# Layer 3: inverse deviations by way of 128 partitions, and one minus the offset's size on ScalarE

## The chip, the cores and the metric

The kernel runs on one core of a Trainium2 chip. The metric is the device time of one execution in microseconds (us), as the median of several runs. The engines are named as in the profile: PE (TensorE), PEld (its weight loads), DVE (VectorE), ACT (ScalarE), POOL (GpSimd) and SP (SyncE, which here issues transfers only).

## What is computed

Four layers run one after another on a tensor of 8 images, 256 channels and 32 x 32 pixels: an attention block with an MLP (layer 0), a bottleneck with a deformable convolution (layer 1), a binarised convolution with a batch normalisation (layer 2), and a second deformable convolution block (layer 3). The change touches layer 3 alone. In the reference (cut):

```python
h = silu(bn(conv2d(x, w_cv1, 1, 1), ...))                 # 3x3, 256 -> 128 channels
t = conv2d(h, w_dw, 1, 1, groups=128) + b_dw              # depthwise 3x3
t = gelu(layernorm(t over the 128 channels, ln_g, ln_b))  # (t - mean) * rsqrt(var + eps) * g + b
value = h @ w_inp + b_inp
offset = t @ w_off + b_off                                # 4 groups x 9 taps x (x, y)
mask = softmax(t @ w_msk + b_msk over the 9 taps)
o = dcnv3_core(value, offset, mask)                       # bilinear samples of value, weighted by mask
return x + silu(bn(o @ w_out + b_out))
```

## The kernel before

Channels lie on the 128 partitions, pixels along the free dimension. Layer 3 works image by image (b = 0 to 7), and each image in two halves of 512 pixels (h = 0, 1).

**The front of an image.** The normalised output of layer 2 is added to x and copied into a padded tile. PE convolves it (`convolve3`, 18 taps a half, L1284), ACT applies SiLU (`silu`, L1289). The depthwise convolution is one tap on ACT (`depthwise`, L1307) and eight on DVE (L1310). For the layer norm PE subtracts the mean by a matmul (`centered`, L1319), ACT squares and copies (L1325, L1327), and PE sums the squares in `variances` (L1333): four matmuls put the variances of 256 pixels each on 32 equal rows, so that the tile `rs` (128 x 256) holds 1024 different numbers, each 32 times. ACT takes the root (`deviations`, L1339), DVE the reciprocal of the whole tile (`inverse`, L1342). PE spreads rows 0, 32, 64 and 96 of it over all channels (`inverse_spread`, L1348; `pick` is zero for the other rows), DVE multiplies (`scaled`, L1352), ACT applies GELU (`gelu`, L1355). PE makes offsets and masks (`offsets3`, L1361), and DVE adds their bias (L1368).

**From offsets to weights.** No pixel is gathered. Offsets here are below 1 in size, so a bilinear sample is a sum over the 3 x 3 pixels around the tap, and with the 9 taps over 25 shifts. `hats` makes the three hat functions of an offset: its absolute value (ACT, L1380), the positive parts of both signs (ACT, L1382, L1384), the largest absolute value for a final test that offsets are indeed below 1 (DVE, L1386), and one minus the absolute value (DVE, L1388). `masks` is the softmax (L1400 to L1409; exponentials on ACT). `weights` multiplies and adds them up into 25 weights per pixel and group: `mx`, `pt`, `ws` on POOL (L1421, L1424, L1427), for image 0 on DVE. `parts` splits them into three bf16 parts (ACT L1438, DVE L1436), PE transposes them (L1447), ACT copies (L1452).

**The products.** For each half and each of the 25 shifts PE spreads a weight over the channels (`shift_weights`, `pw`, L1457, three PSUM banks), DVE multiplies it with the shifted values (`product`, `pr`, L1466, six buffers), and the products are added up: most on POOL (`add_pool`, L1481 for the first addition of a half and L1483), the others on PE (`add_helper`, L1475) or DVE (L1471). The two sums meet in `add_both` (`ab`, DVE, L1486). `outward` (PE, L1490), SiLU (`outward_silu`, ACT, L1495), `add_input` (`oi`, POOL, L1500) and a store on SP (L1503) end the half.

**What sets the order.** A planner in the kernel, `Order`, sets the order of the work on all engines when the program is built. Each piece has an engine, an estimated time, a rank, the pieces that it comes after, the buffers that it takes and gives, and a lag until another engine sees its end. The planner takes whichever piece can start first by these estimates, and of several the one with the lowest rank; a switch of ACT's function table counts 1.28 us. PE, ACT, DVE and POOL then execute in exactly this order, each waiting at its next instruction until what it needs is there; SP executes its transfers in order too. The pieces around the change read:

```python
piece(("dev", b), "ACT", 0.48, r, [("var", b)], deviations, b, give=["ps"], kind="sqrt")
piece(("inv", b), "DVE", 1.74, r, [("dev", b)], inverse, b)
for h in range(2):
    piece(("is", b, h), "PE", 0.86, r, [("inv", b)], inverse_spread, b, h, take=["ps"])
    piece(("sc", b, h), "DVE", 0.68, r - 500, [("is", b, h), ("zc", b, h)], scaled, b, h, give=["ps"])
```

Here r is 100 b; the products have rank 100 b + 150.

Layer 0 has transfers within SBUF of a like kind, to which the prediction turns for a price: `lay` (L499) copies a row block of sums to other partitions, and L436 puts small blocks of eight rows into one row.

Of the kernel before, what the change touches and what calls it, by code (L numbers as in the profile page):

```python
# [8 lines left out]
F32 = mybir.dt.float32  # L9
# [3 lines left out]
AF = mybir.ActivationFunctionType  # L13
ALU = mybir.AluOpType
# [4 lines left out]
P = 128  # L19
# [31 lines left out]
QP = N // 4  # L51
# [107 lines left out]
def conv_seq_kernel(ctx: ExitStack, tc: tile.TileContext, d: dict, out: bass.AP):  # L159
    nc = tc.nc  # L160
# [75 lines left out]
    with ExitStack() as s0:  # L236
        w = s0.enter_context(tc.tile_pool(name="a_w", bufs=1))
# [343 lines left out]
        for n, m in enumerate(blocks):  # L581
            b, g, h = m
# [79 lines left out]
    with ExitStack() as s1_:  # L662
        w = s1_.enter_context(tc.tile_pool(name="b_w", bufs=1))
# [42 lines left out]
        one = s1_.enter_context(tc.tile_pool(name="b_one", bufs=1))  # L706
# [15 lines left out]
        def piece(key, engine, time, rank, after, f, *args, take=(), give=(), lag=Order.LAG):  # L722
            T[key] = work.add(engine, time, rank, [T[a] for a in after if a in T], lambda: f(*args), take, give, lag)
# [315 lines left out]
        for b in range(B):  # L1039
            r = 100 * b  # L1040
# [18 lines left out]
            r = 100 * b - 50  # L1059
# [51 lines left out]
        b = B - 1  # L1111
# [21 lines left out]
        b = B - 1  # L1133
        for o in range(2):
            piece(("vu", o), "PE", 3.9, 100 * b + 330, [("x", b, 0, 0), ("x", b, 1, 0), ("h", b, 1, 7)], convolve_upper, b, o, 0, take=["pm"])
        for h in range(2):
            for o in range(2):
                k = b, o, h
                r = -200 + 10 * h + o
# [21 lines left out]
    with ExitStack() as s3_:  # L1161
        w = s3_.enter_context(tc.tile_pool(name="d_w", bufs=1))
# [30 lines left out]
        identb = w.tile([P, P], BF16, name="identb")  # L1193
        group = w.tile([P, G3], F32, name="group")
        silu_in = w.tile([P, 1], F32, name="silu_in")

        def constants():
            nc.vector.tensor_scalar_add(center, ident, -1.0 / P)
            nc.vector.memset(mean_w, 1.0 / P)
            nc.vector.memset(pick, 0.0)  # L1200
            for j in range(4):
                nc.vector.memset(pick[32 * j : 32 * j + 1, j % 2, :], 1.0)
            nc.vector.tensor_copy(identb, ident)
# [9 lines left out]
        one = s3_.enter_context(tc.tile_pool(name="d_one", bufs=1))  # L1213
# [29 lines left out]
        T, S = {}, {}  # L1243
# [93 lines left out]
        def deviations(b):  # L1337
            S["rs", b] = one.tile([P, QP], F32, name="rs")
            nc.scalar.activation(S["rs", b], S.pop(("var", b))[:, :QP], AF.Sqrt, bias=eps)  # L1339

        def inverse(b):
            nc.vector.reciprocal(S["rs", b], S["rs", b])  # L1342

        def inverse_spread(b, h):
            S["is", b, h] = bank3()
# [27 lines left out]
        def hats(b, i):  # L1373

            off = S["om", b][:, :, : 2 * GK]
            if i == 0:
                S["hat", b] = one.tile([P, 3, NT, 2 * GK], F32, name="hat")
            hat = S["hat", b]
            if i == 0:
                nc.scalar.activation(hat[:, 1], off, AF.Abs)  # L1380
            elif i == 1:
                nc.scalar.activation(hat[:, 0], off, AF.Relu, scale=-1.0)  # L1382
            elif i == 2:
                nc.scalar.activation(hat[:, 2], off, AF.Relu)  # L1384
            elif i == 3:
                nc.vector.tensor_reduce(largest[:, b : b + 1], hat[:, 1].rearrange("p t o -> p (t o)"), AX.X, ALU.max)  # L1386
            else:
                nc.vector.tensor_scalar(hat[:, 1], hat[:, 1], -1.0, 1.0, ALU.mult, ALU.add)  # L1388

        def masks(b, i):  # L1390

# [113 lines left out]
        for b in range(B):  # L1505

            r = 100 * b
# [6 lines left out]
            if b == 0:  # L1514
                piece("arrange", "DVE", 1.7, 20, [("a", 0, 1, 1)], arrange)
                piece("constants", "DVE", 2.0, 20, [("a", 0, 1, 1)], constants)
                for i in range(SB):
                    piece(("sel", i, 0), "DVE", 0.4, 60, ["constants"], spread_rows, i, 0, take=["spread"])
                    piece(("sel", i, 1), "PE", 0.25, 60, [("sel", i, 0)], spread_rows, i, 1, take=["ps"], give=["spread"])
                    piece(("sel", i, 2), "DVE", 0.25, 60, [("sel", i, 1)], spread_rows, i, 2, give=["ps"])  # L1520
                piece("silu", "ACT", 0.2, r, [("xp", 0, 1)], nc.scalar.activation, silu_in, eps, AF.Silu, kind="silu")
            last = ("c", b - 1, 1, 1, 8)
            for h in range(2):
                for t in range(2):
                    for k in range(9):
                        c = b, h, t, k
# [15 lines left out]
                piece(("zc", b, h), "ACT", 0.6, r, [("zs", b, h)], centered_copy, b, h, 1, give=["ps"])  # L1542
            piece(("var", b), "PE", 0.8, r, [("zs", b, 0), ("zs", b, 1)], variances, b, take=["ps"])
            piece(("dev", b), "ACT", 0.48, r, [("var", b)], deviations, b, give=["ps"], kind="sqrt")
            piece(("inv", b), "DVE", 1.74, r, [("dev", b)], inverse, b)
            for h in range(2):
                piece(("is", b, h), "PE", 0.86, r, [("inv", b)], inverse_spread, b, h, take=["ps"])
                piece(("sc", b, h), "DVE", 0.68, r - 500, [("is", b, h), ("zc", b, h)], scaled, b, h, give=["ps"])
# [8 lines left out]
            piece(("ms", b, 4), "DVE", 0.8, r, [("ms", b, 3)], masks, b, 4)  # L1557
            for i in range(3):
                piece(("ha", b, i), "ACT", 0.67, r, om + [("ha", b, i - 1)], hats, b, i)
            piece(("ha", b, 3), "DVE", 0.72, r + 90, [("ha", b, 0)], hats, b, 3)  # L1560
            piece(("ha", b, 4), "DVE", 0.54, r, [("ha", b, 3)], hats, b, 4)
            piece(("w", b, -1), "POOL", 0.9, r, om, weights, b, -1, 0)
            ready = [("ms", b, 4), ("w", b, -1)] + [("ha", b, i) for i in (1, 2, 4)]
            last = []
# [15 lines left out]
            r = 100 * b + 150  # L1580
# [44 lines left out]
    with tc.If(nc.values_load(flag[0:1, 0:1]) > 0):  # L1625
        with ExitStack() as s3_:
            w = s3_.enter_context(tc.tile_pool(name="d_w", bufs=1))
# [25 lines left out]
            one = s3_.enter_context(tc.tile_pool(name="d_one", bufs=1))  # L1653
# [210 lines left out]
```

## Time and profile before

| | us |
|---|---|
| median of 3 runs (4552.45 to 4561.46) | 4553.63 |
| profiled execution: its own time | 4538.69 |
| profiled execution: span of the core | 4536.9 |
| busy in the span: PE / DVE / ACT / POOL | 4030.8 / 3065.7 / 1857.3 / 3300.6 |
| first reciprocal L1342 starts at | 3938.2 |
| first product added on POOL at | 3979.0 |

The profile is of one execution on the core; the mean granted clock of PE was 0.941 of full speed. Layer 3 fills the last 15% or so of the span, from about 3880 us on. A view names an engine, a line of the kernel, the operation and "written <- read" tiles; a number behind an x is a count, an arrow in brackets names what ended the idle time before an instruction. `pr`, `part`, `ws` and so on are names of tiles.

### The profile page before, as it was taken

Reading aid. Unit: us, or ns where it says so; the run is one execution under the profiler, and the core shown is the slowest. Engines: PE = TensorE matmul, PEld = TensorE weight load, DVE = VectorE, ACT = ScalarE, POOL = GpSimd, SP = SyncE. Lnnn points to the kernel's source line nnn. Section 1 sums busy time; section 2 is a strip of 40 time slices with the busy share of each in tenths; the row PEclk is TensorE's granted clock in tenths of the full one; section 3 lists DMA queues with packets and bytes.
Section 4 is the critical chain, followed back from the end, with each engine's and each line's share of the span. In section 5 each row is a group of like instructions: output and inputs, shape, how many; then the busy total and the mean of one; then the engine's idle time right before and its main releaser. Section 6 shows DMA issues by size and latency. Waiting matters only on the chain.

```text
span 4536.9 us, 60173 instructions
## 1 busy us (share of the span) xinstructions
PE 4030.8 (89%) x20901; PEld 1551.4 (34%) x20901; DVE 3065.7 (68%) x5201; ACT 1857.3 (41%) x3338; POOL 3300.6 (73%) x2011
## 2 busy tenths in 40 slices
PE   6999999999999999999999998777777766899977
PEld 2333333333333333333333323322233322344332
DVE  6777777777777777777777763455464554688885
ACT  2554555555555555555455542122122211534331
POOL 3889888988888888988898873554554653078787
PEclk8999999999999999999999999887788888999988
DMA  5212222222221221222222211222332332100000
GB/s 163 66 57 58 65 65 54 65 71 56 59 72 55 61 71 55 58 67 64 55 63 74 57 49 52 80 83 73 88 89 66 99 103 66 40 10 15 14 14 24
DMA packets 207143, 283.09 MB, mean 62 GB/s; under 512 B 87264, under 2 KB 117488, under 8 KB 206576
## 3 DMA queue, kind: packets, MB, share of 16 engines
q1 hardware_dynamic: 176272, 195.46, 15.4%
q0 software_dynamic: 28720, 77.90, 5.8%
q10 hardware_dynamic: 1840, 5.81, 0.3%
q8 instruction: 168, 2.75, 0.3%
q14 instruction: 143, 1.17, 0.1%
HBM read 181.07 MB, written 63.82 MB: 54 GB/s over the span
## 4 chain that ended last, share of the span: by engine, by line
PE 68%; DVE 13%; another core or an unknown queue 7%; issue 5%; POOL 5%; ACT 2%; DMA 1%; SPq 0%; DVEq 0%; POOLq 0%; ACTq 0%
PE av L460 19%; PE pb L403 11%; PE sc L448 10%; PE pb L386 5%; PE pc L1284 3%; PE pm L758 3%; PE pb L534 2%; PE po L771 2%; PE pb L330 2%; DVE near_p L935 2%; POOL part L1483 2%; PE pc L1006 2%; DVE pm L407 1%; DVE r L491 1%
## 5 line engine op out<-in xcount | busy, mean ns | idle before, releaser
L470 POOL TENSOR_TENSOR esum<-esum,e 128x1024 f32<-128x1024 f32 x762 | 1809.2, 2405 | 54.6 <-ACT e L449 54.1
L407 DVE TENSOR_REDUCE pm<-pb 128x1 f32<-128x512 f32 x2016 | 1357.3, 685 | 657.0 <-PE pb L403 653.1
L449 ACT ACTIVATE e<-sc 128x512 f32<-128x512 f32 x2048 | 1056.9, 602 | 676.3 <-PE sc L448 664.1
L460 PE MATMUL av<-e,v 128*64 128x512 f32 x4096 | 1053.4, 593 | 0.0
L913 POOL DMA_INDIRECT g<-table,idx x576 | 550.2, 955 | 562.1 <-DVE near_p L935 286.5
L403 PE MATMUL pb<-sk,sq 128*64 128x512 bf16 x4032 | 772.7, 387 | 56.3 <-DVE x L542 23.4
L448 PE MATMUL sc<-q,k 32*128 32x512 f32 x4096 | 592.9, 642 | 0.0
L403 PEld LDWEIGHTS <-sq 128*64 128x64 bf16 x4032 | 266.2, 109 | 911.0 <-issue 885.6
L468 POOL TENSOR_TENSOR esum<-e 128x1024 f32<-128x1024 f32 x127 | 303.1, 2406 | 299.0 <-ACT e L449 299.0
L460 PEld LDWEIGHTS av<-e,v 128*64 128x64 f32 x4096 | 294.7, 137 | 208.7 <-issue 117.7
L1483 POOL TENSOR_TENSOR part<-part,pr 128x512 f32<-128x512 f32 x212 | 276.1, 1302 | 54.6 <-DVE pr L1466 43.3
L771 PE MATMUL po<-hid,kept 128*128 128x512 f32 x512 | 257.6, 653 | 57.0 <-DVE x L775 41.9
L1466 DVE TENSOR_TENSOR pr<-pw,v 128x512 f32<-128x512 f32 x394 | 253.9, 682 | 63.5 <-POOL part L1483 31.8
L1284 PE MATMUL pc<-xpad,kept 128*128 128x512 f32 x576 | 276.1, 603 | 11.6 <-ACT xpad L1279 8.0
L758 PE MATMUL pm<-y,wide 128*128 128x512 f32 x512 | 247.8, 631 | 27.8 <-ACT hid L763 20.5
L534 PE MATMUL pb<-o,wp 128*64 128x512 f32 x1024 | 245.0, 597 | 1.2 <-DVE r L512 0.6
L448 PEld LDWEIGHTS sc<-q,k 32*128 32x128 f32 x4096 | 166.0, 183 | 230.1 <-issue 186.0
L386 PE MATMUL pb<-wide,y 128*64 128x256 f32 x2048 | 241.8, 379 | 0.0
L491 DVE RECIPROCAL r<-r 128x128 f32<-128x128 f32 x252 | 237.3, 942 | 0.1
L763 ACT ACTIVATE hid<-pm,vec 128x512 f32<-128x512 f32 x128 | 86.8, 686 | 284.5 <-PE pm L758 146.5
L935 DVE TENSOR_TENSOR near_p<-g,near_p 128x320 f32<-128x320 f32 (+1 forms) x384 | 177.4, 462 | 13.2
L390 ACT COPY v<-pb 128x512 f32<-128x512 f32 x128 | 75.1, 586 | 265.5 <-PE pb L386 265.5
(265 smaller groups left out, 4068.8 us busy)
## 6 DMA issues: line engine op xcount, KB each, us to landing
sq<-lev_d SPq DMA_DIRECT2D x512, 64.0 KB
r<-r SPq DMA_DIRECT2D x504, 64.0 KB
sk<-lev_d SPq DMA_DIRECT2D x496, 64.0 KB
lev_d<-lev SPq DMA_DIRECT2D x180, 128.0 KB
u_d<-u SPq DMA_DIRECT2D x60, 256.0 KB
g<-table,idx POOLq DMA_INDIRECT x576
out<-res SPq DMA_DIRECT2D x32, 256.0 KB
q<-u_d SPq DMA_DIRECT2D x124, 64.0 KB
```

Of the source, the lines that this page charges most:

```text
L386: nc.tensor.matmul(ps[c * 64 : (c + 1) * 64, (mt % 2) * 256 : (mt % 2 + 1) * 256], ys[b][:, t, k0 : k0 + 64], wv[:, t, g * 256 : (g + 1) * ...
L403: nc.tensor.matmul(ps[c * 64 : (c + 1) * 64, :], sq[pair][:, c, q0 : q0 + 64], sk[pair][:, c, kh * HALF : (kh + 1) * HALF], start=True, st ...
L407: nc.vector.tensor_reduce(maxima[m][:, pair, qt, kh : kh + 1], ps, AX.X, ALU.max)
L448: nc.tensor.matmul(ps, k[r, kt * P : (kt + 1) * P], q[r, h * HALF : (h + 1) * HALF], start=True, stop=True)
L449: nc.scalar.activation(es[m, kt, j // 2][:, j % 2, :], ps, AF.Exp)
L460: nc.tensor.matmul(av[i * HD : (i + 1) * HD, :], vss[b, g][:, kt, j * HD : (j + 1) * HD], e[:, i, :], start=kt == 0, stop=kt == NT - 1,)
L470: eng.tensor_add(sums[m, pair], sums[m, pair], es.pop((m, kt, pair)))
L758: nc.tensor.matmul(ps, w1[:, t, i * P : (i + 1) * P], ys[b, h][:, t, :], start=t == 0, stop=t == 1)
L771: nc.tensor.matmul(pss["o", b, h, t], w2[:, j, t * P : (t + 1) * P], hids[b, h, j], start=j == 0, stop=j == 7)
L913: nc.gpsimd.indirect_dma_start(out=g[:, k, :], out_offset=None, in_=tables[b][:TR, :], in_offset=bass.IndirectOffsetOnAxis(ap=idxs[b][:, t ...
L1284: nc.tensor.matmul(S["c", b, h], wc[:, t, k, :], tap(xpads[t], k, H // 2, h * H // 2), start=t == k == 0, stop=t == 1 and k == 8,)
L1483: nc.gpsimd.tensor_add(S["part", b, h], S["part", b, h], S.pop(("pr", b, h, on_pool[n])))
```

## The change

Two things change. First, the reciprocal of the deviations. `narrow` copies rows 0, 32, 64 and 96 of `rs`, each 256 numbers on one partition, onto 32 partitions of 8 numbers each (`r8`, 128 x 8), in four transfers on SP's queue. DVE takes the reciprocal of `r8`. `widen` copies the results back into the four rows, again in four transfers. Second, one minus the absolute offset is made by ACT instead of DVE, with a bias tile of ones. Ranks change with it: the new pieces have r - 500, and the maximum of the offsets has r instead of r + 90. The lines of the changed kernel lie 2 to 14 further down.

```diff
+        unit = w.tile([P, 1], F32, name="unit")
...
+            nc.vector.memset(unit, 1.0)
...
+        def narrow(b):
+            S["r8", b] = one.tile([P, QP // 32], F32, name="r8")
+            for j in range(4):
+                nc.sync.dma_start(S["r8", b][32 * j : 32 * j + 32, :], S["rs", b][32 * j : 32 * j + 1, :].rearrange("o (p c) -> o p c", p=32))
+
         def inverse(b):
-            nc.vector.reciprocal(S["rs", b], S["rs", b])
+            nc.vector.reciprocal(S["r8", b], S["r8", b])
+
+        def widen(b):
+            for j in range(4):
+                nc.sync.dma_start(S["rs", b][32 * j : 32 * j + 1, :].rearrange("o (p c) -> o p c", p=32), S["r8", b][32 * j : 32 * j + 32, :])
...
-                nc.vector.tensor_scalar(hat[:, 1], hat[:, 1], -1.0, 1.0, ALU.mult, ALU.add)
+                nc.scalar.activation(hat[:, 1], hat[:, 1], AF.Identity, bias=unit, scale=-1.0)
...
-            piece(("inv", b), "DVE", 1.74, r, [("dev", b)], inverse, b)
+            piece(("nar", b), "SP", 0.5, r - 500, [("dev", b)], narrow, b, lag=2.2)
+            piece(("iv", b), "DVE", 0.15, r - 500, [("nar", b)], inverse, b)
+            piece(("inv", b), "SP", 0.5, r - 500, [("iv", b)], widen, b, lag=2.2)
...
-            piece(("ha", b, 3), "DVE", 0.72, r + 90, [("ha", b, 0)], hats, b, 3)
-            piece(("ha", b, 4), "DVE", 0.54, r, [("ha", b, 3)], hats, b, 4)
+            piece(("ha", b, 3), "DVE", 0.72, r, [("ha", b, 0)], hats, b, 3)
+            piece(("ha", b, 4), "ACT", 0.6, r, [("ha", b, 3)], hats, b, 4)
```

Since the planner plans with these costs, the order of the pieces around them changes on all engines.

## The prediction

> **What bounds the kernel now.** The page puts layer 3 at the end of the span. I read the windows first, then POOL's and DVE's waits within the stage, then the changed lines, then the timeline of the first batch. Windows (columns: us, then busy us and instructions of PE, PEld, DVE, ACT, POOL, then granted clock):
>
> ```profile
> 4060.00:4120.00 60.00, 58.24 (x210) 27.18 (x208) 54.79 (x80) 25.91 (x33) 49.13 (x42) 1.00 0.03 9
> 4300.00:4360.00 60.00, 51.20 (x171) 22.30 (x172) 52.12 (x79) 23.47 (x29) 50.95 (x41) 0.94 0.05 18
> ```
>
> Three engines are 80 to 97% busy, ACT under half: nothing is free except on ACT. Waits of POOL and DVE, 3940 to 4537 us:
>
> ```profile
> POOL part L1481 <- DVE pr L1466: 115.3, 12, 91.5
> POOL part L1483 <- DVE pr L1466: 43.3, 48, 4.3
> ...
> DVE pr L1466 <- POOL part L1483: 31.8, 19, 11.6
> DVE pr L1466 <- PE pw L1457: 29.2, 50, 2.3
> ```
>
> 91.5 us is POOL's wait for its first product; after it POOL waits 23.8 + 43.3 = 67 us for DVE, and DVE 32 us for POOL. The bound changes hands: sometimes DVE's products are late (POOL idle 2 to 4 us), sometimes POOL adds 14 in a row and DVE waits for a buffer. The two changed lines (min/median/max ns):
>
> ```profile
> L1342 DVE RECIPROCAL rs<-rs x8: 1742/1743/1752, 3938.2 to 4383.0; 128x256 f32<-128x256 f32 x8
> ...
> L1388 DVE TENSOR_SCALAR hat<-hat x8: 460/962/1171, 3948.5 to 4425.3; 128x576 f32<-128x576 f32 x8
> ```
>
> Batch 0, timeline (start, us). Its reciprocal finds DVE idle, and the chain from it leads to the first product and so to POOL's start:
>
> ```profile
> 3937.66 0.47 ACT L1339 ACTIVATE rs<-ps,eps 128x256 f32<-128x256 f32 x1
> ...
> 3938.17 1.75 DVE L1342 RECIPROCAL rs<-rs 128x256 f32<-128x256 f32 x1 [3.57 <-ACT rs L1339]
> ...
> 3940.24 1.14 PE L1348 MATMUL ps<-rs,pick 64*128 64x256 f32 x8
> ```
> ```profile
> 3978.99 1.27 POOL L1481 TENSOR_TENSOR part<-pr 128x512 f32<-128x512 f32 x1 [91.53 <-DVE pr L1466]
> ```
>
> Layer 3 makes no such transfer, but layer 0 does: row to rows (L499) and rows to row (L436). Timeline of SP, then of POOL, which uses the last L499 transfer:
>
> ```profile
> 2376.97 2.80 SPq L436 DMA_DIRECT2D q<-line  x4
> ...
> 2686.44 4.94 SPq L499 DMA_DIRECT2D r<-r  x8
> ```
> ```profile
> 2692.98 1.27 POOL L504 TENSOR_TENSOR o<-r,o 128x512 f32<-128x512 f32 x1 [0.79 <-DMA r<-r]
> ```
>
> Four transfers of this kind cost SP 2.80 us of issue, and the reader starts 2692.98 - (2686.44 + 4.94) = 1.60 us after the last issue ends. So four together land about 4.4 us after SP may start.
>
> **What the Trainium skill says.** "DMA: Bandwidth & Descriptors", section "Anatomy of one DMA", gives a fixed part of about 2.0 us per DMA on GpSimd's path, most of it the receipt of the write. The trace's 1.60 us after the issue agrees in kind, and I use the trace. "VectorE: DVE Perf Modes", section "First, the fixed hardware budget", has the reciprocal as an iterated divide; the trace agrees: 1743 ns / 256 columns = 6.8 ns each, a product 681 / 512 = 1.3 ns. "SBUF — State Buffer", section "SBUF: two separate sides", says that DVE and GpSimd take an exclusive lock on a shared port pair for certain operations; L1388 took 460 ns in batch 0, where POOL was idle, and up to 1171 later, which fits. "ScalarE: Activation LUTs", section "Table sets: the hidden batching unit", lists identity in every table set; L1300, an Identity, runs in the trace without a load of its own.
>
> **The change part by part.** I read the order of instructions of both kernels, engine by engine.
>
> 1. DVE loses 8 x 1.743 = 13.9 us of reciprocals and the eight L1388, 7.3 us in sum. It gains eight reciprocals of 8 columns. Their price from two rows: 128x256 takes 1743 ns, 128x32 (L1407) 350 ns, so 6.2 ns a column and about 0.2 us for 8; bounds 0.06 and 0.35. Net -19.6 us, of which batch 0 (some 2 us) was idle anyway: **-17.6 us of DVE work in batches 1 to 7**, 2.5 us of the some 52 busy in each window of 60 above.
> 2. ACT gains 8 x 0.67 us (the price of L1382, same shape) and has one table load fewer in the stage (1.28 us). It is 40% busy: nothing, while `mx` on POOL waits for other work. If that cover were gone, 0.67 us a batch.
> 3. The path from deviations to spread was one reciprocal, 1.74 us. It is now narrow 4.4 + 0.2 + widen 4.4 = **9.0 us**, against 0.5 + 2.2 us for each transfer in the planner's costs. Trace of before can't show a 32-byte-row transfer: 2.7 to 5.0 us each are my bounds, 4.4 the value taken.
> 4. Batch 0: IS (L1348) moves from 3940.24 to 3938.13 + 9.0 = 3947.1, **+6.9 us**. No DVE work is queued there, and masks, weights, turned weights and the first product hang on it. PE has 7 convolution taps instead of 3 between variances and spread, then stands (queued behind: the taps of batch 1). 4 x 0.86 = 3.4 us of PE work is thus done ahead and partly repaid when PE's taps next hold DVE up (DVE waits 6.4 us at 4015 us for such a silu). I take +5.5 us; bounds +2 and +7.
> 5. Batches 1 to 7: waits in DVE's queue. Before, the reciprocal started 0.97, 1.09, 4.1, 5.9, 1.8, 4.5, 4.8 us after the deviations. With products (0.61 us a step) moved ahead of or behind it by the new order, DVE gets there after about 2.8, 2.9, 6.0, 6.5, 2.4, 4.5, 2.9 us, and the data after 4.4: waits of 1.6 + 1.5 + 0 + 0 + 2.0 + 0 + 1.5 = 6.6 us. Then `scaled` needs widen (4.4) and the first spread (0.6); the products and adds in between are worth 3.1, 3.1, 4.4, 4.4, 2.4, 1.8, 3.7 us: waits of 1.9 + 1.9 + 0.6 + 0.6 + 2.6 + 3.2 + 1.3 = 12.1 us. Queued behind both waits are products, which POOL and PE wait for; behind the spread on PE, the shift weights `pw`. Sum 18.7 us, about the 17.6 us that DVE is relieved of. Where POOL adds 14 in a row (4152.9, 4301.6, 4371.8 us) six product buffers hide both. I take +1 us for this part; -11 if no wait shows, +9 if relief falls where POOL bounds and waits where DVE does.
> 6. In batches 3 to 7 the maximum (L1386, 0.74 us) moves ahead of the sum `ab` and the next half's first products, for which L1481 on POOL then waits 2.0 to 4.3 us each: 5 x 0.74 = +3.7 us; 0 if the product moved behind it pays it back.
> 7. SP carries 64 more issues, 5.6 us per batch. In its queue narrow stands behind the stores of an earlier half. For batch 2 the last such addition on POOL ended at 4055.3 and the deviations came at 4057.8; ACT's new order puts the deviations after that half's silu. I take 0; a late POOL would cost up to 3 us once or twice.
>
> Sum: 5.5 + 1 + 3.7 = **+10 us**. On the profiled execution (span 4536.9, its own time 4538.7) that is 4548.9. The median of the runs shown is 4553.6, 15 us above that execution, so the forecast against the median is 4553.6 + 10 = **4564 us**.
>
> **The rivals.**
> - *Relief wins* (faster). The mechanism: DVE's 17.6 us come off POOL's 67 us of waits for products, and the new waits fall in the stretches where POOL bounds. For it: seven of the eight reciprocals sit among products, and POOL waited 1 to 2.5 us around 4243 us, where DVE was full. Against: three stand next to POOL's unbroken rows of adds. Price: -17.6 with the front's +5.5 and little else: -12 us, 4542. It decides if a group of transfers lands within about 3 us rather than 4.4, since the waits of step 5 then fall from 18.7 to about 4 us.
> - *Paid back*: the front's delay is real, but DVE gets back 6 us in the stretches where it bounds. 4553, no change. For it: both sums of step 5 are near each other.
> - *Queue of SP*: narrow waits for stores as in step 7 and spreads hold PE, 3 us in three batches on top: +19, 4573. It is my case, worse.
> - *It doesn't do what it says*: the reciprocal would be on 128 partitions and still not short, if its cost were fixed. The 350 ns of 32 columns speaks against it.
>
> **How the numbers follow.** About 0.2%, 9 us, is what a measurement of this kernel can tell from no change. Slower by over that: +10 and the SP case, 0.44. Within: 0.23. Faster: relief wins, 0.33, as the order of all four engines moves and half of DVE's gain is easily kept. The likeliest case alone runs from 4556 (step 5 at -7 us) to 4572 (step 5 at +9). For 8 in 10 the range must take in the middle of relief wins and the SP case: 4540 to 4580.
>
> **What would show it.** In the changed profile: deviations to first spread about 9 us in every batch; POOL's first add about 6 us later than 3979 us; waits of DVE for the transfers of some 6 us, and for the spread of some 12; DVE's busy time down by about 20 us; the time from POOL's first add to the end longer by some 4 us. Wrong: spread under 6 us after the deviations, or POOL's 67 us of waits for products down by 10 or more.

## The result and the profile after

| | before | after |
|---|---|---|
| median of five runs, us | 4557.61 (4552.45 to 4561.46) | 4580.05 (4572.88 to 4584.68) |
| profiled execution: its own time / span, us | 4538.69 / 4536.9 | 4572.88 / 4571.0 |
| busy DVE / POOL in the span, us | 3065.7 / 3300.6 | 3043.5 / 3298.6 |
| start of the deviations of batch 0 to the end of the span, us | 599.2 | 624.5 |
| of it up to POOL's first addition, us | 41.3 | 46.0 |

The ratio is 1.005, with an interval of 1.0036 to 1.0065: the change costs 22.4 us. The forecast was +10. Of the 34 us between the two spans, 25.3 lie in layer 3, from the deviations of batch 0 on. The other 8.9 lie ahead of it and belong to the two executions rather than to the change: e11 below, which is the kernel before with two buffers more, reaches the deviations at 3951.3 us, later than the change at 3946.5.

DVE did 22 us less work, as the forecast had it, and the kernel became slower. The timelines of batch 0, of ACT, SP, DVE, PE and POOL in this order (start, duration, engine, line, idle time in brackets), show the new path:

```profile
3946.52 0.47 ACT L1341 ACTIVATE rs<-ps,eps 128x256 f32<-128x256 f32 x1
```
```profile
3947.02 2.48 SPq L1347 DMA_DIRECT2D r<-rs  x4
3950.99 2.44 SPq L1354 DMA_DIRECT2D rs<-r  x4
```
```profile
3950.76 0.20 DVE L1350 RECIPROCAL r<-r 128x8 f32<-128x8 f32 x1 [7.30 <-DMA r<-rs]
```
```profile
3953.66 2.14 PE L1360 MATMUL ps<-rs,pick 64*128 64x256 f32 x8
```
```profile
3992.55 1.27 POOL L1493 TENSOR_TENSOR part<-pr 128x512 f32<-128x512 f32 x1 [97.60 <-DVE pr L1478]
```

The deviations end at 3946.99, the short reciprocal starts at 3950.76, and the first spread at 3953.66: narrow takes 3.8 us, and 6.7 us pass from the deviations to the spread. POOL's first addition comes 46.0 us after the start of the deviations instead of 41.3.

The waits within the stage, 3940 to 4571 us (engine, tile and line waiting <- what it waited for: us in total, times, longest):

```profile
POOL part L1493 <- DVE pr L1478: 115.7, 13, 97.6
POOL part L1495 <- DVE pr L1478: 68.4, 63, 5.9
```
```profile
DVE pr L1478 <- POOL part L1495: 48.6, 11, 12.4
DVE pr L1478 <- PE pw L1469: 40.3, 63, 2.9
DVE r L1350 <- DMA r<-rs: 17.1, 6, 7.3
...
DVE wide L1364 <- PE ps L1360: 8.8, 8, 3.9
```

After its first product POOL waited for products 18.1 + 68.4 us, against 67 before, though DVE had less to do. DVE's own wait for POOL grew from 31.8 to 48.6 us. Eleven waits make these 48.6 us, and four of them make 44.8: 11.16, 11.58, 9.60 and 12.41 us. The kernel before had two of this size, 10.10 and 11.56. In both kernels the last one is in the last batch and has no depthwise taps behind it. So the change has three with taps behind them, before had one.

This is the second of the three, in the timelines of DVE, POOL and PE:

```profile
4306.52 2.48 DVE L1478 TENSOR_TENSOR pr<-pw,v 128x512 f32<-128x512 f32 x4
4308.92 1.53 DVE L1312 SCALAR_TENSOR_TENSOR pd<-h,vec,pd 128x512 f32<-128x512 f32 x2
4322.03 0.69 DVE L1478 TENSOR_TENSOR pr<-pw,v 128x512 f32<-128x512 f32 x1 [11.58 <-POOL part L1495]
4322.64 0.74 DVE L1312 SCALAR_TENSOR_TENSOR pd<-h,vec,pd 128x512 f32<-128x512 f32 x1
4323.42 0.75 DVE L1312 SCALAR_TENSOR_TENSOR wide<-h,vec,pd 128x512 f32<-128x512 f32 x1
4325.07 5.50 DVE L1312 SCALAR_TENSOR_TENSOR pd<-h,vec,pd 128x512 f32<-128x512 f32 x7 [0.91 <-ACT pd L1309]
4330.61 0.75 DVE L1312 SCALAR_TENSOR_TENSOR wide<-h,vec,pd 128x512 f32<-128x512 f32 x1
```
```profile
4304.37 0.79 POOL L1433 TENSOR_TENSOR mx<-hat,mask 128x288 f32<-128x288 f32 x1
...
4318.24 2.54 POOL L1439 TENSOR_TENSOR ws<-ws,pt 128x288 f32<-128x288 f32 x3
4320.73 7.99 POOL L1495 TENSOR_TENSOR part<-part,pr 128x512 f32<-128x512 f32 x6
4333.01 2.62 POOL L1495 TENSOR_TENSOR part<-part,pr 128x512 f32<-128x512 f32 x2 [4.29 <-DVE pr L1478]
```
```profile
4308.80 1.02 PE L1487 MATMUL pa<-pr,ident 128*128 128x512 f32 x2
```

From 4304.4 to 4320.7 POOL makes weights (`mx`, `pt`, `ws`) and adds no product. DVE makes products 4 to 11 of the half (counted from 0) and then has product 12 next in its queue. It stands until POOL has added one more product, number 5, at 4322.0. Right behind it in the queue are ten taps of the depthwise convolution (L1312), which need no product buffer. They run after the stop, when POOL wants products, and POOL runs dry for 4.29 us. So 11.6 us are lost in which DVE could have done the taps, 7.7 us of work, and the taps then take time from products.

The PE line shows the odd part. In this half PE adds products 1, 4, 7 and 10, and the last of these additions ended at 4309.8. From then on a buffer was free, and product 12 waited all the same. The planner and the memory disagree here. In the planner `pr` is a count of six, and any product that is added gives one back: in its plan (us of the plan) PE's addition of product 10 ends at 407.1, product 12 starts at 408.1, ahead of the taps, and POOL's addition of product 5 ends only at 418.0. In memory a product gets a certain one of the six buffers when the program is built. By the addresses in the built program of the change, product 12 has the buffer of product 5, which POOL adds, and the one that PE freed is kept for product 14. So it isn't that the planner took POOL to be faster than it is: by its own times product 12 would have stood 10 us for the buffer that it got.

The expectations below call this the turn: the buffers are taken to go round in the order in which they were given out. That is nearly so, not quite. In the change 242 of 388 products have the buffer of the product six before, the others that of one 1 to 10 before; product 11 above had that of product 7. How the build chooses is not shown.

The kernel before has the same picture once:

```profile
4226.60 0.69 DVE L1466 TENSOR_TENSOR pr<-pw,v 128x512 f32<-128x512 f32 x1 [10.10 <-POOL part L1483]
```

### The profile page after: what moved, and what is told of

The parts are those of the page before. It is cut to its first block, busy times and chain, and to the rows that moved or that the text cites. A ratio compares the mean times of both kernels' runs of the same rounds, so it can differ in the third digit from the quotient of the medians.

```text
span 4571.0 us, 60302 instructions
## 1 busy us (share of the span) xinstructions
PE 4012.9 (88%) x20901; PEld 1548.5 (34%) x20901; DVE 3043.5 (67%) x5194; ACT 1860.3 (41%) x3345; POOL 3298.6 (72%) x2011
## 4 chain that ended last, share of the span: by engine, by line
PE 69%; DVE 13%; another core or an unknown queue 6%; issue 5%; POOL 4%; ACT 2%; DMA 1%; SPq 0%; DVEq 0%; POOLq 0%; ACTq 0%
PE av L460 19%; PE pb L403 11%; PE sc L448 10%; PE pb L386 5%; PE pc L1286 3%; PE pm L758 3%; PE pb L534 2%; PE po L771 2%; PE pb L330 2%; PE pc L1006 1%; DVE pm L407 1%; DVE near_p L935 1%; DVE r L491 1%; PE pb L481 1%
## 5 line engine op out<-in xcount | busy, mean ns | idle before, releaser
L1495 POOL TENSOR_TENSOR part<-part,pr 128x512 f32<-128x512 f32 x212 | 272.9, 1287 | 78.7 <-DVE pr L1478 68.4
L1478 DVE TENSOR_TENSOR pr<-pw,v 128x512 f32<-128x512 f32 x394 | 253.7, 683 | 92.6 <-POOL part L1495 48.6
L1469 PE MATMUL pw<-wT,sel 120*128 120x512 bf16 (+1 forms) x400 | 136.5, 397 | 64.9 <-DVE pr L1478 64.8
```

## The experiments

The theory, **stops**: with other pieces and costs the planner's order falls more often into a place where a product waits for a buffer that POOL still holds, though by the plan's count one is free, with taps behind it. The expectations call it the full ring, and later the turn. Rivals: the new waits behind transfers; the maximum's rank; and, later, simply too few buffers.

The runs were made in five sets, and a median is compared with the kernel before in the same set. In e9 to e12 that takes about 4550 us, as in the result, in the others about 4203; the change itself was run only where before takes 4550. The difference lies ahead of the part that matters here: the deviations of batch 0 start at 3946 to 3953 us in e9 to e12 and at 3600 to 3608 in the others. So the time from there to the end, "the stage" below, can be compared across the sets, with the reserve that it is of one profiled execution each.

All runs in one table; "stops" counts waits of DVE of over 8 us for a product's buffer with taps queued right behind:

| run | what it is | stops | us against before | ratio, interval |
|---|---|---|---|---|
| e1 | hat on ACT and the maximum's rank, no transfers | 5 | +38.9 | 1.0077 to 1.0111 |
| e2 | transfers alone | 1 | +4.0 | 1.0005 to 1.0019 |
| e3 | the change's order, no transfers, long reciprocal | 3 | +18.9 | 1.0027 to 1.0061 |
| e4 | the change's order, eight buffers | 0 | -0.2 | 0.9994 to 1.0012 |
| e5 | transfers in the order of before | 1 | +30.3 | 1.0051 to 1.0085 |
| e6 | the maximum's rank alone | 2 | +19.4 | 1.0028 to 1.0062 |
| e7 | hat on ACT alone | 1 | -3.0 | 0.9981 to 0.9998 |
| e8 | the change, rings of 6 and 2 | 0 | +1.0 | 0.9995 to 1.0013 |
| e9 | the change | 3 | +24.8 | 1.0037 to 1.0070 |
| e10 | the change, the maximum's old rank | 4 | +29.3 | 1.0042 to 1.0086 |
| e11 | before, eight buffers | 0 | -4.4 | 0.9983 to 1.0004 |
| e12 | hat on ACT, rings of 6 and 2 | 0 | -3.8 | 0.9990 to 1.0005 |
| e13 | the change, rings of 4 and 2 | 0 | -1.6 | 0.9988 to 1.0006 |
| e14 | the change, turns in the plan | 0 | -0.7 | 0.9990 to 1.0007 |
| e15 | before, turns in the plan | 0 | -8.6 | 0.9971 to 0.9988 |
| e16 | hat on ACT, eight buffers, turns in the plan | 0 | -8.4 | 0.9969 to 0.9987 |
| e17 | e14, no transfers in batch 0 | 0 | +1.0 | 0.9993 to 1.0010 |
| e18 | e17, transfers planned longer | 0 | -7.4 | 0.9973 to 0.9988 |

### Which part costs (e1 to e3)

e1 is before with `hats` 4 on ACT and `r` for the maximum; e2 is the change without these two; e3 is the change, its plan and its order kept, with these lines:

```diff
-            nc.vector.reciprocal(S["r8", b], S["r8", b])
+            nc.vector.reciprocal(S["rs", b], S["rs", b])
...
-            piece(("nar", b), "SP", 0.5, r - 500, [("dev", b)], narrow, b, lag=2.2)
+            piece(("nar", b), "SP", 0.5, r - 500, [("dev", b)], lambda *_: None, b, lag=2.2)
```

(and the same for `widen`).

> The kernel before with only the second part of the change: one minus the offset's size on ScalarE, the maximum at rank r; the reciprocal stays whole on DVE. Theory 'full ring' (the loss of the change is a product planned ahead of depthwise taps while all six product buffers are full and POOL makes weights, so that DVE stands 10 to 12 us with the taps behind it): it depends on where the new plan puts the products; with two or more such stops it is slower by 5 us or more, with at most the one stop of before within 6 us of before. Theory 'transfers' (the loss is DVE's and PE's wait for the eight transfers a batch): no transfers, so 0 to -7 us against before. Theory 'maximum ahead of the products': +3 us.

> The changed kernel with only its first part: the reciprocal by way of 128 partitions; one minus the offset's size back on DVE with the old ranks. Theory 'full ring': as with the other half, slower by some 7 us for each stop of DVE over 8 us with taps behind it beyond the one of before. Theory 'transfers': all of the +22 us or more. Theory 'maximum ahead of the products': some 4 us less than the change.

> The changed kernel with exactly its planned order on all engines, but the two groups of transfers are left out and DVE takes the whole reciprocal (1.74 us) in the place of the short one. Theory 'full ring': still slower than before, by some 13 to 18 us (the change's 22 less the front's 5), with the same three long stops of DVE. Theory 'transfers': back to before or faster, 0 to -5 us.

e1, which has none of the transfers, is the slowest of all, +39 us. e2, which has them all, costs 4 us, and its first addition on POOL comes 46.0 us after the start of the deviations, as in the change. e3 makes no transfer, does the long reciprocal, and is still 19 us slower. So most of the loss is in the order and not in the transfers. e1 has five stops with taps behind, of 10.1 to 11.6 us, e3 three of 9.6 to 11.6 us at the change's places, e2 one of 10.7.

### The same order with eight buffers (e4)

```diff
-        gp = s3_.enter_context(tc.tile_pool(name="d_g", bufs=6))
+        gp = s3_.enter_context(tc.tile_pool(name="d_g", bufs=8))
```

The planner still counts six, so every engine's order is that of the change.

> The changed kernel, its order unchanged (the planner still counts six), but with eight product buffers in place of six. Theory 'full ring': the stops of 10 to 12 us vanish or shrink below 3 us, the taps run while POOL makes weights, and the time falls by 12 us or more, to within 10 us of before. Theory 'transfers': as the change, +18 to +25 us, because the waits for transfers stay.

The waits of DVE and POOL in it:

```profile
DVE pr L1478 <- POOL part L1495: 6.9, 6, 3.0
```
```profile
POOL part L1495 <- DVE pr L1478: 37.6, 44, 2.5
```

The stops are gone, POOL's wait falls from 68.4 to 37.6 us, and the kernel is as fast as before. That the loss arose at the stops can be read half by half. These are the sums (`ab`) that end the sixth and the eleventh half, first in the change, then in e4:

```profile
4215.44 0.68 DVE L1498 TENSOR_TENSOR part<-pa,part 128x512 f32<-128x512 f32 x1
...
4426.80 0.68 DVE L1498 TENSOR_TENSOR part<-pa,part 128x512 f32<-128x512 f32 x1
```
```profile
3867.71 0.68 DVE L1498 TENSOR_TENSOR part<-pa,part 128x512 f32<-128x512 f32 x1
...
4056.68 0.69 DVE L1498 TENSOR_TENSOR part<-pa,part 128x512 f32<-128x512 f32 x1 [2.27 <-POOL part L1495]
```

The change takes 211.4 us from one to the other, e4 189.0. These 22.4 us come in three steps of 6.0, 9.5 and 6.8 us, in the seventh, ninth and eleventh half, where the three stops of 11.2, 11.6 and 9.6 us lie. From POOL's first addition to the end the two kernels differ by 25.2 us in all (21.2 with e9 for the change). With the order of every engine unchanged, the buffers account for nearly the whole loss.

### The remaining suspects one at a time (e5 to e7)

e5 keeps before's order: one piece `inv` at DVE's place and planned cost (1.74 us) makes narrow, short reciprocal and widen one after another, so nothing is planned to cover the transfers.

```diff
+        def inverse(b):
+            narrow(b)
+            inverse8(b)
+            widen(b)
...
+            piece(("inv", b), "DVE", 1.74, r, [("dev", b)], inverse, b)
```

> The kernel before with its planned order on PE, ACT, DVE and POOL, but in the place of each whole reciprocal the four narrow transfers, the short reciprocal and the four widen transfers, without any cover planned for them. Theory 'full ring': the long stop of DVE stays the one of before, so what this costs is the bare latency: the front's 4 to 5 us plus 2 to 3 us for each batch in which DVE waits with nothing to do, less 1.5 us of DVE work a batch; +5 to +15 us. Theory 'transfers' (they make the loss of the change): +20 us or more.

It cost 30 us, with the stops of before and no more. That is twice the most that "full ring" allowed and lies where "transfers" had it. Waits of DVE, PE and POOL:

```profile
DVE wide L1366 <- PE ps L1362: 20.7, 12, 4.5
...
DVE r L1347 <- DMA r<-rs: 14.9, 5, 7.3
```
```profile
PE ps L1362 <- DMA rs<-r: 17.6, 9, 4.2
```
```profile
POOL part L1497 <- DVE pr L1480: 61.2, 47, 5.5
```

So the transfers do cost much where nothing is planned between them. In the change, whose plan counts them, DVE's waits for spread and narrow are 8.8 and 17.1 us; e2, at +4 us, shows that most of their cost is then covered.

e6 changes one rank in before, `("ha", b, 3)` from `r + 90` to `r`; e7 moves the hat to ACT in before and leaves the rank.

> The kernel before with one number changed: the maximum of the offsets at rank r in place of r + 90; one minus the offset's size stays on DVE. Theory 'rank': it is this reordering that makes the second part slow, so +25 to +40 us with four or more stops of DVE over 8 us. Theory 'lighter DVE': the stops come from taking 7 us of work off DVE, so within 8 us of before.

> The kernel before with one minus the offset's size on ScalarE, the maximum still at rank r + 90. Theory 'lighter DVE': +25 to +40 us with four or more stops of DVE over 8 us that have depthwise taps or part subtractions behind them. Theory 'rank': within 8 us of before, or up to 7 us faster.

One rank, of a piece of 0.74 us, costs 19 us, less than expected and with fewer stops. It leads to stops of 11.90, 8.24 and 11.49 us, the last two with taps right behind. They are not all of its cost. POOL also waits for masks, which it doesn't do in before:

```profile
POOL mx L1421 <- DVE mask L1409: 22.7, 7, 5.8
```

The hat on ACT alone gives 3 us. So the rank can lead to stops; whether it is their cause in the change was left to e10.

### More memory, in two ways (e8 to e12)

e8 and e12 give the products that PE or DVE adds two buffers of their own, in the plan and in memory:

```diff
-                dst = S["pr", b, h, s] = gp.tile([P, HALF], F32, name="pr")
+                dst = S["pr", b, h, s] = (gq.tile([P, HALF], F32, name="pq") if s in on else gp.tile([P, HALF], F32, name="pr"))
```

e9 is the change as it is, e10 the change with the maximum at `r + 90` again, e11 before with eight buffers.

> The changed kernel with the product buffers split in two rings, six for the products that POOL adds and two for those that PE or DVE add, in the planner's count as in the memory. The theory behind the stops: the planner takes a product's buffer to be any free one of six, but buffers go round in turn, and the seventh product waits for the oldest even where PE has freed younger ones. If that is so, plan and chip agree here: no stop of DVE over 5 us with taps behind it, and the time is at or below that of eight buffers in one ring, 0 to -15 us against before. If the stops come from a wrong estimate of POOL's time instead, stops of over 8 us remain and the time is +5 us or more.

> The changed kernel itself, to stand beside the others on the same chip. Both theories: +18 to +26 us against before, as at first.

> The changed kernel with the maximum of the offsets back at rank r + 90; transfers and ScalarE's part as in the change. Theory 'rank and ring' (the rank makes the plans with long stops of DVE, the transfers alone cost 5 us, ScalarE's part gains 5): within 8 us of before, at most one stop of DVE over 8 us with taps behind it. Theory 'transfers and lighter DVE together': +15 us or more.

> The kernel before, its order unchanged, with eight product buffers in one ring in place of six. Theory 'full ring': one stop of 10 us with taps behind it goes, -3 to -10 us. If the buffers alone bring a gain everywhere, -20 us, as the changed kernel's drop from six to eight.

> The kernel before with one minus the offset's size on ScalarE (old rank, no transfers) and the product buffers in two rings of six and two, in the plan as in the memory. A version meant to beat both: theory 'full ring': -8 to -16 us against before, no stop of DVE over 5 us with taps behind it. If only the order decides by chance, anything from -10 to +15 us.

e8 has no stop and costs nothing that can be told from noise; the gain of up to 15 us that was allowed for didn't come. e9 confirms the result (+25 us). e10 ends the theory of the rank: with the old rank the change has four stops of 10.2 to 10.4 us and costs 29 us, more than with the new one. So the rank alone doesn't decide; each edit shuffles the order, and how often that ends in a stop looks like chance, which these runs can't prove. e11 and e12 bring no gain that the medians can tell from none, and the 8 to 16 us expected of e12 didn't come. In the profiled executions, though, the stage of e11 is 9.0 us shorter than that of before (590.2 against 599.2), and 8.2 of these lie in the seventh half, where before has its stop. So that stop costs some 8 us by the traces, and between nothing and 8 by the medians.

### Too few buffers, or a plan that counts them wrongly (e13 to e16)

All versions without stops so far had more memory. e13 splits the six buffers into four and two. e14 leaves one ring of six and changes only the planner: a product may start only when the product six before it has been added. That isn't the memory's rule exactly, but it is stricter than a count of any six; below it is the rule of the turn. e15 is before with this rule, e16 before with the rule, the hat on ACT and eight buffers.

```diff
+                        if r in self.turn:
+                            i = len(self.taken[r]) - self.turn[r]
+                            start = max(start, self.released.get(self.taken[r][i], float("inf")) if i >= 0 else 0.0)
+                            continue
```

> The change, with its six product buffers in two rings: four for the products that POOL adds, two for those that PE or DVE adds, in the plan and in memory alike. Theory 'turn' (the stops come from a plan that takes any free buffer of six while memory takes them in turn): no wait of a product over 5 us with taps queued behind it, and -10 to +8 us against the kernel before. Theory 'too few buffers': stops of about 10 us as in the change, and +12 us or more.

> The change, with one ring of six as it has; the planner alone differs: a product may start only when the one six before it has been added up. Theory 'turn': no wait of a product over 5 us with taps behind it, since taps are now planned into that time, and -10 to +8 us against the kernel before. Theory 'too few buffers': the same stops, and +12 us or more.

> The kernel before with the same rule in its planner. Theory 'turn': its one stop with taps behind it (10 us) goes, worth up to 8 us of it: -8 to +3 us. Theory 'too few buffers': nothing changes in the waits, 0 us, or slower where the rule holds products back.

> The kernel before with one minus the offset's size on ScalarE, eight product buffers, and the rule of the turn in the planner. The reciprocal stays on DVE, whole. Theory 'turn': no stop, and DVE is 7 us lighter: -5 to -15 us against the kernel before. Theory 'too few buffers' gives the same stops-free picture here. If lighter DVE work is worth nothing while POOL bounds: -4 to 0 us, as with eight buffers alone.

With six buffers and a stricter plan the stops are gone and the 25 us with them, in both forms. In e14 the taps lie where the stop was (timeline of DVE, then POOL, whose weights start at 3946.2):

```profile
3949.97 3.91 DVE L1325 SCALAR_TENSOR_TENSOR pd<-h,vec,pd 128x512 f32<-128x512 f32 x5
3953.91 0.75 DVE L1325 SCALAR_TENSOR_TENSOR wide<-h,vec,pd 128x512 f32<-128x512 f32 x1
3955.57 5.50 DVE L1325 SCALAR_TENSOR_TENSOR pd<-h,vec,pd 128x512 f32<-128x512 f32 x7 [0.91 <-ACT pd L1322]
3961.11 0.75 DVE L1325 SCALAR_TENSOR_TENSOR wide<-h,vec,pd 128x512 f32<-128x512 f32 x1
```
```profile
3964.10 21.40 POOL L1508 TENSOR_TENSOR part<-part,pr 128x512 f32<-128x512 f32 x15
```

DVE does fourteen taps while POOL makes weights, and POOL then adds fifteen products without a pause, where in the change it stopped after six. DVE's waits for POOL before a product are 0.4 us in sum. "Too few buffers" falls. e15 and e16 are faster than both kernels, 8.6 and 8.4 us under before. e16's lighter DVE and two more buffers add nothing to the rule of the turn that these runs show.

### Where the last 8 us lie (e17, e18)

e14 takes 7.9 us longer than e15, both without stops. e17 takes the transfers out of batch 0 alone; e18 also counts each group of transfers at 3.7 us.

```diff
-                piece(("nar", b), "SP", 0.5, r - 500, [("dev", b)], narrow, b, lag=2.2)
+                piece(("nar", b), "SP", 0.5, r - 500, [("dev", b)], narrow, b, lag=3.2)
```

> The change with the turn in the planner, but batch 0 takes its reciprocal of the whole tile on DVE as in the kernel before; batches 1 to 7 keep the transfers. Theory 'front' (the delay of batch 0 reaches the end in full): POOL's first addition 41.3 us after the deviations again instead of 46.0, and about 4197, -4 to -7 us against the kernel before. Theory 'front is paid back': no more than 2 us gained on e14, -3 to 0 us against the kernel before.

> As e17, and the planner counts each group of transfers at 3.7 us instead of 2.7, which is what the trace shows. Theory 'waits behind transfers cost': the waits of DVE for narrow and for the spread in batches 1 to 7, about 10 us in sum, shrink under 4 us, and the kernel gains 2 to 4 us on e17. Theory 'such waits are covered, since POOL has products in store': within 1.5 us of e17.

e17 went against "front". Its first addition came 41.3 us after the start of the deviations again, 4.7 us earlier than in e14, and it ended no earlier: from the first addition to the end it took 557.4 us, e14 551.2. What was won there was lost later, 4.4 of the 6.2 us by the end of the fourth half. e18 took 546.7 us for that part and gained 8.4 us on e17, more than expected, but not for the expected reason: DVE's waits for narrow and spread went from 7.1 + 6.1 to 5.1 + 5.8 us, 2.3 us in all. POOL's waits for products fell by more (first e17, then e18):

```profile
POOL part L1509 <- DVE pr L1492: 45.8, 57, 3.9
```
```profile
POOL part L1509 <- DVE pr L1492: 37.9, 54, 3.0
```

POOL is busy for nearly the same time from its first addition to the end in all of these, 450 to 452 us, so what differs is how long it stands: 100.9 us in e14, 94.2 in e15, 106.8 in e17, 95.8 in e18. None of its waits for a product after the first exceeds 4.3 us there. DVE still has longer waits, but not for a product: each of the four stands 14 to 15 us in the last batch for a copy by ACT, where no taps are left, and e17 alone stands 11.7 us for such a copy in the first half:

```profile
3684.24 1.15 DVE L1462 TENSOR_TENSOR ws<-ws,parts 128x800 f32<-128x800 f32 x1 [11.73 <-ACT parts L1464]
```

Whether this wait starts e17's loss was not tested. The medians of plans without stops spread over some 10 us (-8.6 to +1.0), and what decides among them stays open. e18 has all that the change does in batches 1 to 7 and is within 2 us of e15, which has nothing of it.

## Why the forecast was right in direction and short in size

- **Step 1, DVE's work:** right. Busy time fell by 22.2 us in the span (19.6 forecast). The short reciprocal takes 0.20 us as taken:

```profile
L1350 DVE RECIPROCAL r<-r x8: 192/203/203, 3950.8 to 4415.6; 128x8 f32<-128x8 f32 x8
```

- **Step 2, ACT:** the hat takes 0.76 us there instead of 0.67; e7 shows that it costs nothing, it gave 3 us.
- **Step 3, the path:** too long. 6.7 us from deviations to spread in batch 0 instead of 9.0 (6.4 to 9.5 in the others, where engines are busy). The price came from four transfers of layer 0; here a group lands 3.8 us after the deviations end, and the first half's spread needs only two of the four of widen: it starts 0.23 us after the last of the four has been issued.
- **Step 4, the front:** right in size. POOL's first addition came 4.7 us later by the deviations, +5.5 forecast. That this reaches the end in full is not shown (e17).
- **Step 5, waits against relief:** the waits were near: 9.8 us for narrow (6.6 forecast) and 4.9 for the spread (12.1) in batches 1 to 7, 14.7 against 18.7. That they about cancel the relief agrees with the versions without stops: e4 stands at -0.2 us, e14 at -0.7. But here is the step that failed, in the sentence that "six product buffers hide both". It took six buffers as a store that anyone may refill, as the planner does. In memory a product can stand for a buffer that POOL holds while one that PE has freed lies idle, and the new order put products ahead of taps at three such places instead of one. The step gave its part +1 us and had no term for a wait of DVE for POOL with other work behind it; the three stops took 22 us of the stage (the change against e4), two of them more than before had.
- **Step 6, the maximum's rank:** the term was mis-sized and its mechanism wrong. 0.74 us a batch, +3.7 us, was the price of the piece itself. e6 shows that the same rank can cost 19 us by way of the order, in stops and in POOL's waits for masks, and e10 that going back on it can cost more again.
- **Step 7, SP's queue:** right, no cost was seen. In batch 0 the first of the four transfers starts 0.03 us after the deviations end.

The account by the profiled executions, for the 25.3 us that the stage grew: 4.7 us lie ahead of POOL's first addition. Counted from that addition, the change falls behind before by 3.7 us over the first six halves, by 1.6 in the seventh, where both have a stop, by 10.7 in the ninth and 6.1 in the eleventh, where only the change has one; the other halves give 1.6 back. So some 17 us stand at the two stops that before doesn't have.

Without stops on either side the change stands 4 us (e4 to e11) to 8 us (e14 to e15) above before by medians, 9 and 10 us by the stage; the forecast for these parts was +10. So the forecast's sum fits in size what the transfers, the rank and the front cost in such plans, and what it lacks are the stops.

That the direction came out right is in part luck. The forecast was made against the kernel before as it is, with its own stop. Against that the change without stops stands at -1.6 to +1.0 us (e4, e8, e13, e14): it came out slower only by the stops, which the forecast didn't have.

The sign was in view before. Of the 31.8 us in the line that the forecast showed for DVE's wait for POOL, 21.7 were just two waits. The forecast put them down to POOL's long rows of additions. The place of the first, at 4226.6, was the end of a weights phase, with ten taps queued behind a product; the other is in the last batch and has none.

The rivals: "relief wins" didn't come, since POOL's waits rose. "Paid back" describes the change without stops (e4, e8, e13, e14). The queue of SP gave the right size, +19, for a wrong reason. That the reciprocal would not become short was refuted by its 0.20 us.

## What to carry to other kernels

Where a planner writes the order, a small edit is first of all a new order. Before the edit is judged, look for single long waits in the traces of both kernels and count them; a total hides them. A count of free buffers is not enough for a plan: the buffer that a piece gets is settled when the program is built, and a consumer that is late can hold it while others have long released theirs. Either give each consumer its own ring, or let the plan wait for the older buffers too; here that was worth more than the edit itself. Then an in-order engine's queue decides what a wait costs: ask what independent work stands behind it.

## What was not expected

- Four transfers between one row and 32 rows of 8 numbers, started together by SP, took 2.48 us of issue, and their reader started 3.8 us after the data were there. That is less than for the four of layer 0 in the forecast, with 4.4 us.
- A reciprocal of 8 columns took 0.20 us against 1.74 us for 256; that is 25 ns a column instead of 6.8, which gives an estimate of about 0.15 us for a fixed part.
- The same program and order, with two buffers more of 2 KB a partition, stood at -0.2 us against before, where the change itself stood at +22 and +25 (e4, the result, e9). No engine had less work: busy time doesn't show what an order loses.
